# A Perceiver layer on one core: the last unit's maxima turned to rows on TensorE, the last tile's attention quarters one step apart, the last pair's groups together, and the maximum later in its step

## The chip, the cores and the metric

The kernel runs on one core of a Trainium2 chip. The metric is device time in microseconds (us) of one execution, as the median of several. The core's engines are named as the profile names them: PE is TensorE's matmul, PEld its weight load (which runs beneath the matmul before it), DVE is VectorE, ACT is ScalarE, POOL is GpSimd, and SP is the engine that issues most DMAs here. PSUM is the memory into which PE writes.

## The reference

The layer takes x (16 batches of 64 rows, 256 wide) and a context of 16 batches of 1601 rows, 256 wide. Three residual parts follow one another:

```python
x = x + xattn(layernorm(x), ctx)   # 16 query heads and 8 key groups of 128, self and cross attention
x = x + attn(layernorm(x))         # 16 heads of 16, blocks of 8 rows, causal; then a gated feed-forward
x = x + ffn(layernorm(x))          # ternary weights, 704 wide
```

Most of the arithmetic is the cross attention of the first part, for each batch and each key group:

```python
kvx = cond @ w_kv_x.T; kx, vx = split(kvx)
kx  = ln(kx)                              # per head of 128
xout = softmax(qx @ kx.T / sqrt(128)) @ vx
cat  = concat([core, xout])               # core: self attention over the 64 rows
out  = fp8(clip(bf16(cat / proj_smooth))) @ wproj.T * scale
```

The second part quantises activations per row to 8 bits (`act_quant`: the row's largest magnitude, scale by 127, round) and weights to -1, 0, 1. Its attention works in blocks of 8 rows over 16 heads.

## The kernel before

**Tiles and units.** The 1024 rows of x are 8 tiles i of 128 rows (two batches each), held in SBUF for the whole run as `xr[i]`. The cross attention of a tile is cut into four units: two halves hh of the key groups (four groups each) by two batches bb. So there are 32 units, n = 0 to 31. A unit walks over the context in 13 chunks c of 128 rows (the last 65).

**A unit.** Per chunk, `project` makes the keys `ps_k` (4 matmuls, L487), ACT squares them, `squares` sums the squares per head on DVE (L498) and takes the inverse root on POOL, `normalise` scales into `kn` (DVE, L506), `transpose_k` turns them on PE (`tr_kx`, L520) and evicts them with the norm's weights into `kT` (ACT, L522), and `score` multiplies with the queries (8 matmuls, `s`, L533). The scores have context rows on the partitions and 4 x 128 queries along the row. ACT copies them, scaled, to an SBUF tile `P` (L538), and DVE keeps the running maximum of all chunks in `M` (L541 for the first chunk, L543 after it). There is one buffer of M, and 19 of P, in the pool `pp`.

After the last chunk, `maximum` finds each query's maximum over the context rows, which lie on the partitions: PE transposes M in four blocks (`tr_m`, L550), DVE reduces each (`red`, L552), and DVE scales it (L562). The result stands one query per partition, but it is wanted along the row and on every partition. So SP writes `red` to a DRAM tile `rowd` (L557), and `maximum_in` reads it back to all partitions as `mx` (L567). Then `exponent` subtracts mx from each P (DVE, L571) and takes the exponential in place (ACT, L575), and `accumulate` multiplies P with the context rows and a column of ones (10 matmuls, `acc`, L590). After its last chunk four tiles of the accumulator are divided by their sums into `pq` (L600 to 604), and `turn_contexts` transposes those into the pair's `pc` (`tr_pc`, L613).

**Behind the units.** When both batches of (i, hh) are done, `pair_out` multiplies with the value weights (`po_x`, L645), for two groups gp one after the other; for each it rounds on DVE to fp8 (L654 and the helper at L192 to L197, `cat` L265) and projects (`po_p`, L278), adding into `xr[i]` (L282). Between the two groups it waits for `gap` steps and loads the second group's weights. When tile i's x is complete, `last_parts` runs the second and third residual part of that tile: norm, `act_quant`, the 8-bit qkv product (`ps_qk`, `ps_v`), rope (r1, r2), a transpose to `qkT`, then four *quarters* (two row halves j of heads by two sets c), each with a masked query tile `qm` (L802), scores `sc` (L809), mask and maximum and exponential (L814 to 821), `tr_p` (L825), its ACT copy `pT` (L827), and the value product `av` (L831) into `cx`; then `po_o`, the gated feed-forward (`ps_g`, `ps_u`, `po_d`), and the ternary one (`pgu`, L906, `sgc`, `hd`, and `po_f`, L924), and the output DMA (L931). qm and pT share 2 buffers (`b2b`), sm3 has part of 3 (`b2`).

**What sets the order.** The program is emitted by a hand-written planner. Each piece of work is put on a heap at a step and a rank, `spawn(step, rank, generator)` or `at(step, rank, function)`. The heap hands out by step, then by rank; a generator that yields k continues k steps later at its rank. Every engine runs its own instructions in the order of emission, and waits are placed by dependency. SP's DMAs are also issued in that order. A unit's base is 13n. Within one step s:

- rank 0 the loads, rank 0.5 `maximum_in` (at base + 17), rank 1 normalise
- rank 2 project, rank 2.5 `last_parts` and the quarters, **rank 3.4 `maximum`** (at base + 15)
- rank 3.5 accumulate (c at base + c + 20), rank 4 self attention, queries and norms of the coming tile, rank 4.2 squares
- rank 5 score (c at base + c + 2), rank 6 transpose_k, rank 7 pair_out, rank 8 exponent (c at base + c + 18)

All transposes, scores, projections and quarters share three PSUM tiles of the tag "s". Tile i starts `last_parts` at step 52i + 92, the last one at 52i + 79; its quarters stand three steps apart.

Of the kernel before, what the change touches and what calls it, by code (L numbers as in the profile page):

```python
# [14 lines left out]
F32 = mybir.dt.float32  # L15
# [8 lines left out]
P = 128  # L24
# [34 lines left out]
def body(tc, ctx, a):  # L59
# [28 lines left out]
    def at(step, rank, fn):  # L88
        def once():
            fn()  # L90
            yield 1

        spawn(step, rank, once())
# [89 lines left out]
    def quant_tile():  # L183
        return qp.tile([P, 512], F32, tag="q_y", name="q_y")
# [74 lines left out]
    def to_cat(y, exact):  # L259

        cat = qp.tile([P, 4, P], F32R if exact else F32, tag="cat", name="cat")

        def emit(t, m):
            for g in range(2):
                V.tensor_tensor(  # L265
                    cat[:, 2 * g : 2 * g + 2, :].rearrange("p h (b s) -> p b h s", b=2),
                    t[:, 256 * g : 256 * (g + 1)].rearrange("p (b h s) -> p b h s", b=2, h=2),
                    m[:, 256 * g : 256 * (g + 1)].rearrange("p (b h s) -> p b h s", b=2, h=2), ALU.subtract,
                )

        fp8_round(y, emit)
        return cat
# [191 lines left out]

    def unit(i, hh, bb, base):
        b = 2 * i + bb
        st = {"cxT": {}, "cxN": {}, "ps": {}, "ss": {}, "rs": {}, "kn": {}, "kT": {}, "P": {}, "pT": {}}
        pair = pairs.setdefault((i, hh), {})

# [85 lines left out]
        def out_rows(r):  # L555
            d = dram.tile([4, P], F32, tag="rowd", name="rowd", bufs=4)
            nc.sync.dma_start(out=d.rearrange("g q -> q g"), in_=r)  # L557
            return d

        def maximum():  # L560
            r = turned("M", ALU.max)
            V.tensor_scalar(r, r, C_ATT, None, ALU.mult)  # L562
            st["mxd"] = out_rows(r)

        def maximum_in():
            st["mx"] = one.tile([P, 4, P], F32, tag="mx", name="mx", bufs=2)
# [49 lines left out]
        for c in range(NC):  # L616
# [7 lines left out]
            at(base + c + 17, 0, lambda c=c: load_N(c))  # L624
            at(base + c + 18, 8, lambda c=c: exponent(c))
            at(base + c + 20, 3.5, lambda c=c: accumulate(c))
        at(base + 15, 3.4, maximum)
        at(base + 17, 0.5, maximum_in)
        for k in range(2):
            at(base + 33, 1.8 + 4.4 * k, lambda k=k: turn_contexts(k))  # L630

    def pair_out(i, hh, gap):


        pair = pairs[i, hh]
        wv = piece("wvx", (v2, w_kvT[:, :, 1024 + 512 * hh : 1536 + 512 * hh]))
        yield 1
        w_p = weights("wproj", 4 + 2 * hh)
        yield 1
        for gp in range(2):  # L640
            po = s_tile("po_x")
            for g2 in range(2):
                g = 2 * gp + g2
                for k in range(2):
                    PE.matmul(  # L645
                        po[:, g2 * 256 : (g2 + 1) * 256], lhsT=v2(wv)[:, k, g * D : (g + 1) * D],
                        rhs=pair["pc"][:, k, g].rearrange("p b q -> p (b q)"), start=k == 0, stop=k == 1,
                    )
            y = quant_tile()
            for g2 in range(2):  # L650
                h0 = 24 + 8 * hh + 4 * gp + 2 * g2
                yg = y[:, g2 * 256 : (g2 + 1) * 256].rearrange("p (b h s) -> p b h s", b=2, h=2)
                pg = po[:, g2 * 256 : (g2 + 1) * 256].rearrange("p (b h s) -> p b h s", b=2, h=2)
                V.tensor_tensor(yg, pg, rsc[:, h0 : h0 + 2].unsqueeze(1).unsqueeze(3).to_broadcast([P, 2, 2, S]), ALU.mult)  # L654
            cat = to_cat(y, True)
            yield 1
            project_out(i, cat, w_p)
            if gp == 0:
                yield gap - 3
                w_p = weights("wproj", 5 + 2 * hh)  # L660
                yield 2
# [48 lines left out]
    def b2(name):  # L710
        return one.tile([P, 512], F32, tag="b2", name=name, bufs=3)

    def b2b(name):
        return one.tile([P, 512], F32, tag="b2b", name=name, bufs=2)
# [12 lines left out]
    def act_quant(src, w, j):  # L727


        am = small.tile([P, 1], F32, tag="am", name="am")  # L730
        V.tensor_reduce(am, src, AX.X, ALU.max, apply_absolute_value=True)
        V.tensor_scalar(am, am, 1e-5, None, ALU.max)
        sc = small.tile([P, 1], F32, tag="asc", name="asc")
        V.reciprocal(sc, am)
        V.tensor_scalar(sc, sc, 127.0, None, ALU.mult)
        f = small.tile([P, 1], F32, tag="fsc", name="fsc")
        V.tensor_scalar(f, am, wmean[:, j : j + 1], 1.0 / 127.0, ALU.mult, ALU.mult)
        u = b2("aq_u")
        V.tensor_scalar(u[:, :w], src, sc, 127.0, ALU.mult, ALU.min)
        V.tensor_scalar(u[:, :w], u[:, :w], -128.0, ROUND, ALU.max, ALU.add)  # L740
        q = b1("aq_q", BF16)
        V.tensor_scalar(q[:, :w], u[:, :w], ROUND, None, ALU.subtract)
        yield 1
        tr = tr_tile("tr_aq", BF16)
        for k in range(w // P):
            PE.transpose(tr[:, k * P : (k + 1) * P], q[:, k * P : (k + 1) * P], identb)
        qT = b1("aq_t", BF16)
        V.tensor_copy(qT[:, :w], tr[:, :w])
        yield 1
        return qT.rearrange("p (k t) -> p k t", k=4), f  # L750
# [3 lines left out]
    def last_parts(i, start):  # L754
# [41 lines left out]
        yield 1  # L796
        cx = one.tile([P, H], F32, tag="cx3", name="cx3")

        def quarter(j, c):

            qm = b2b("qm").rearrange("p (h t) -> p h t", h=4)
            V.tensor_tensor(  # L802
                qm, qkT[:, j * P : (j + 1) * P].unsqueeze(1).to_broadcast([P, 4, P]),
                hmask[:, 4 * c : 4 * c + 4].unsqueeze(2).to_broadcast([P, 4, P]), ALU.mult,
            )
            yield 1
            sc = s_tile("sc3")
            for h in range(4):
                PE.matmul(  # L809
                    sc[:, h * P : (h + 1) * P], lhsT=qm[:, h, :], rhs=qkT[:, 256 + j * P : 256 + (j + 1) * P],  # L810
                    start=True, stop=True,
                )
            sm = b2("sm3").rearrange("p (h t) -> p h t", h=4)
            V.tensor_tensor(  # L814
                sm, sc.rearrange("p (h t) -> p h t", h=4), cmask.unsqueeze(1).to_broadcast([P, 4, P]), ALU.add
            )
            mx = small.tile([P, 4], F32, tag="mx3", name="mx3")
            V.reduce_max(mx, sm, axis=AX.X)
            V.tensor_tensor(sm, sm, mx.unsqueeze(2).to_broadcast([P, 4, P]), ALU.subtract)
            yield 1  # L820
            A.activation(sm, sm, AF.Exp, scale=0.25)
            yield 1
            tr = tr_tile("tr_p3")
            for h in range(4):
                PE.transpose(tr[:, h * P : (h + 1) * P], sm[:, h, :], ident)  # L825
            pT = b2b("pT3")
            A.copy(pT, tr)  # L827
            yield 1
            av = s_tile("av")
            for h in range(4):  # L830
                PE.matmul(  # L831
                    av[:, h * 17 : (h + 1) * 17], lhsT=pT[:, h * P : (h + 1) * P], rhs=vx[:, 8 * j + 4 * c + h, :],
                    start=True, stop=True,
                )
            av3 = av[:, 0 : 4 * 17].rearrange("p (h d) -> p h d", h=4)
            rv = small.tile([P, 4], F32, tag="rv3", name="rv3")
            V.reciprocal(rv, av3[:, :, 16])
            o = 128 * j + 64 * c
            V.tensor_tensor(
                cx[:, o : o + 64].rearrange("p (h d) -> p h d", h=4), av3[:, :, 0:16],  # L840
                rv.unsqueeze(2).to_broadcast([P, 4, 16]), ALU.mult,
            )

        s0 = start + 9
        for n in range(4):
            spawn(s0 + 3 * n, 2.5, quarter(n // 2, n % 2))
        yield 3 * 3 + 5
        to = ternary_piece(1536, 512).rearrange("p (k o) -> p k o", k=2)
        yield 1
        cT, f = yield from act_quant(cx, H, 1)  # L850
# [101 lines left out]
    for i in range(NT):  # L952
        base = 52 * i
        for hh in range(2):
            for bb in range(2):
                unit(i, hh, bb, base + 26 * hh + 13 * bb)
            spawn(base + 26 * hh + 13 + 34 - 2, 7, pair_out(i, hh, 5 if i < NT - 1 or hh == 0 else 3))
        ln0, sa0, qx0 = SCHEDULE[i] if i in SCHEDULE else (
            base - 23, [base + o for o in (-16, -4, 8, 22)], [base + o for o in (-14, -5, 12, 20)]
        )  # L960
        spawn(ln0, EX, ln_tile(i))
        for p in range(4):
            spawn(sa0[p] - 2, EX, self_attention(i, p))
            spawn(qx0[p] - 2, EX, queries(i, p))
        l0 = base + (92 if i < NT - 1 else 79)
        spawn(l0, 2.5, last_parts(i, l0))
    spawn(60, 5.7, ternary())
    order = [(kind, p) for p in range(4) for kind in ("wq", "wkv", "wqx", "wproj")]
# [75 lines left out]
```

## Time and profile before

Three runs took 2778.85, 2780.6 and 2781.8 us, the median is 2780.6. The profiled execution took 2779.82 us, of which the span from first to last instruction is 2777.7; its mean TensorE clock was 0.978 of full.

| | us |
|---|---|
| median of 3 runs | 2780.6 |
| profiled execution, its span | 2779.82, 2777.7 |
| PE busy, first 100 us | 79.08 |
| PE busy, 100 to 620 | 485.34 of 520 |
| PE busy, 2709.6 to 2739.8 (the last tile's four quarters) | 17.19 of 30.2, clock 0.58 |
| `acc` L590, 4160 matmuls | 807.6 |
| `ps_k` L487, 1664 matmuls | 796.5 |
| `s` L533, 3328 matmuls | 445.9 |
| `M` L543, 384 operations on DVE | 263.4 |
| `mx` subtraction L571, 416 operations on DVE | 282.1 |

A row with a line number sums what the program does there over all 32 units. A stretch such as 100 to 620 is counted from the start of the span. Where a row of the profile is followed by an arrow (`tr_m <- DVE M`), the instruction on the left stood idle until the one on the right had ended.

### The profile page before, as it was taken

The page shows a single profiled execution, that of the slowest core. Times are in us where ns is not written, and L with a number is a line of the kernel's source. Part 1 is how long each engine was busy: PE and PEld are TensorE (multiplying, and loading weights), DVE is VectorE, ACT ScalarE, POOL GpSimd, SP SyncE. Part 2 cuts the span into 40 slices and gives each one's busy share as a digit, 9 for nine tenths or more (in the row PEclk, how much of TensorE's full clock was granted, in tenths as well). Part 3 has the DMA queues.
Part 4 walks back from the last instruction along what each step waited for, and adds up shares of the span by engine and source line. Part 5 has one row for each costly group of instructions (what it writes and reads, how often), then busy time and mean ns, then how long its engine had stood idle before and what let it go on. Part 6 is the DMA issues. An engine that isn't in the chain of part 4 may idle for free.

```text
span 2777.7 us, 41656 instructions
## 1 busy us (share of the span) xinstructions
PE 2623.7 (94%) x14848; PEld 2033.2 (73%) x14848; DVE 1896.1 (68%) x4643; ACT 1418.9 (51%) x2556; POOL 851.0 (31%) x1248
## 2 busy tenths in 40 slices
PE   7899989999999999999999999999999999999885
PEld 4577767768777787777777687777877778777774
DVE  7777756767666766667677676676766676765643
ACT  4555534445565455644556445654556545574421
POOL 3333323332333323333332333323333332333100
PEclk9999999999999999999999999999999999999986
DMA  7556634334344334434344343443434433443220
GB/s 253 187 173 193 229 123 134 101 109 124 110 146 142 117 102 122 133 113 135 117 127 132 97 130 114 145 133 107 120 113 142 142 120 105 118 129 82 64 90 14
DMA packets 232351, 353.34 MB, mean 127 GB/s; under 512 B 43952, under 2 KB 172752, under 8 KB 232144
## 3 DMA queue, kind: packets, MB, share of 16 engines
q1 hardware_dynamic: 231856, 350.52, 40.4%
q8 instruction: 117, 1.92, 0.3%
q14 instruction: 90, 0.74, 0.1%
q10 hardware_dynamic: 288, 0.17, 0.0%
HBM read 327.74 MB, written 22.87 MB: 126 GB/s over the span
## 4 chain that ended last, share of the span: by engine, by line
PE 69%; DVE 17%; POOL 6%; ACT 3%; DMA 3%; issue 2%; SPq 0%; ACTq 0%; POOLq 0%; DVEq 0%
PE acc L590 20%; PE ps_k L487 19%; PE s L533 10%; PE tr_kx L520 5%; DVE ss L498 2%; POOL rs L160 2%; PE po_p L278 2%; DVE M L543 2%; PE po_x L645 2%; DVE P L571 2%; DVE kn L506 1%; POOL rsx L160 1%; PE pgu L906 1%; POOL ve L159 1%; PE ps_q L324 1%
## 5 line engine op out<-in xcount | busy, mean ns | idle before, releaser
L590 PEld LDWEIGHTS acc<-ctxN,P 128*128 128x128 f32 (+1 forms) x4160 | 713.5, 192 | 186.2 <-issue 105.0
L590 PE MATMUL acc<-ctxN,P 128*128 128x257 f32 (+5 forms) x4160 | 807.6, 342 | 8.8 <-ACT pq L602 8.8
L487 PE MATMUL ps_k<-wkx,ctxT 128*128 128x512 f32 (+1 forms) x1664 | 796.5, 599 | 5.8 <-DVE wkx L941 5.4
L159 POOL TENSOR_SCALAR ve<-ss 128x4 f32<-128x4 f32 (+2 forms) x432 | 218.9, 507 | 1493.2 <-DVE ss L498 1275.0
L575 ACT ACTIVATE P<-P 128x512 f32<-128x512 f32 (+1 forms) x416 | 261.2, 630 | 579.7 <-DVE P L571 579.3
L533 PE MATMUL s<-qx,kT 128*128 128x128 f32 (+1 forms) x3328 | 445.9, 277 | 25.4 <-ACT kT L522 8.2
L160 POOL TENSOR_TENSOR rsx<-ve,nhalf 128x4 f32<-128x4 f32 (+1 forms) x416 | 437.7, 1052 | 31.6
L533 PEld LDWEIGHTS s<-qx,kT 128*128 128x128 f32 (+1 forms) x3328 | 406.4, 188 | 44.7 <-ACT kT L522 13.0
L487 PEld LDWEIGHTS ps_k<-wkx,ctxT 128*128 128x128 f32 (+1 forms) x1664 | 282.2, 189 | 204.2 <-issue 194.6
L543 DVE TENSOR_TENSOR M<-s,M 128x512 f32<-128x512 f32 (+1 forms) x384 | 263.4, 686 | 225.4 <-ACT P L538 222.9
L492 ACT ACTIVATE sq<-ps_k 128x512 f32<-128x512 f32 (+1 forms) x416 | 248.3, 597 | 311.3 <-PE ps_k L487 299.6
L498 DVE TENSOR_REDUCE ss<-sq 128x4 f32<-128x512 f32 (+1 forms) x416 | 283.0, 680 | 138.2 <-ACT sq L492 136.5
L522 ACT ACTIVATE kT<-tr_kx,vec 128x512 f32<-128x512 f32 (+1 forms) x416 | 315.9, 759 | 31.8 <-PE tr_kx L520 31.8
L538 ACT ACTIVATE P<-s 128x512 f32<-128x512 f32 (+1 forms) x416 | 246.5, 592 | 147.1 <-PE s L533 145.1
L506 DVE TENSOR_TENSOR kn<-ps_k,rsx 128x512 f32<-128x512 f32 (+1 forms) x416 | 282.8, 680 | 14.9 <-POOL rsx L160 14.9
L571 DVE TENSOR_TENSOR P<-P,mx 128x512 f32<-128x512 f32 (+1 forms) x416 | 282.1, 680 | 10.7 <-DMA mx<-rowd 10.7
L520 PE MATMUL tr_kx<-ident,kn 128*128 128x128 f32 (+1 forms) x1664 | 247.6, 272 | 28.1 <-DVE kn L506 16.7
L520 PEld LDWEIGHTS tr_kx<-ident,kn 128*128 128x128 f32 (+1 forms) x1664 | 192.7, 143 | 38.1 <-DVE kn L506 12.7
L178 DVE TENSOR_SCALAR qn<-qn,mv,rs 128x128 f32<-128x128 f32 x256 | 76.1, 341 | 83.2 <-POOL rs L172 83.1
L160 POOL TENSOR_TENSOR rs<-ve,nhalf 128x4 f32<-128x4 f32 (+2 forms) x144 | 113.7, 790 | 8.3
L278 PE MATMUL po_p<-wproj,cat 128*128 128x256 f32 x512 | 85.5, 310 | 5.5 <-DVE cat L265 5.4
L168 DVE BATCH_NORM_STATS2 st<-qn 128x6 f32<-128x128 f32 x256 | 63.8, 271 | 37.7 <-ACT qn L334 37.7
(187 smaller groups left out, 2599.2 us busy)
## 6 DMA issues: line engine op xcount, KB each, us to landing
wproj<-wproj SPq DMA_DIRECT2D x120, 512.0 KB
ctxT<-in_ctx SPq DMA_DIRECT2D x192, 256.0 KB
ctxN<-in_ctx_n SPq DMA_DIRECT2D x384, 128.0 KB
wq<-wq SPq DMA_DIRECT2D x56, 512.0 KB
wkv<-wkv SPq DMA_DIRECT2D x56, 512.0 KB
wqx<-wqx SPq DMA_DIRECT2D x56, 512.0 KB
mx<-rowd SPq DMA_DIRECT2D x32, 256.0 KB
wvx<-in_w_kv_x SPq DMA_DIRECT2D x16, 512.0 KB
```

What stands on the lines that cost most here:

```text
L160: GP.tensor_tensor(out, ve[:n, :g], nhalf[:n, :g], ALU.pow)
L487: PE.matmul(ps[:n, :], lhsT=st["cxT"][c // 2][:, k, o : o + n], rhs=wkx[:, k, 512 * hh : 512 * (hh + 1)], start=k == 0, stop=k == 1,)
L492: A.activation(sq[:n], ps[:n], AF.Square)
L498: mark["ss"] = V.reduce_sum(ss[:n], st["ss"].pop(c)[:n].rearrange("p (g d) -> p g d", g=4), axis=AX.X)
L506: mark["kn"] = V.tensor_tensor(kn[:n].rearrange("p (g d) -> p g d", g=4), ps[:n].rearrange("p (g d) -> p g d", g=4), rs[:n].unsqueeze(2).t ...
L520: PE.transpose(tr[:, g * P : g * P + n], kn[:n, g * D : (g + 1) * D], ident[:n, :n])
L522: A.activation(kT[:, :, 0:n], tr.rearrange("p (g t) -> p g t", g=4)[:, :, 0:n], AF.Identity, bias=col("kxln_b"), scale=col("kxln_w"),)
L533: PE.matmul(ps[:n, g * P : (g + 1) * P], lhsT=kT[:, g, 0:n], rhs=qxs[i, hh][:, bb, 2 * g : 2 * g + 2, :].rearrange("p h s -> p (h s)"), st ...
L543: mark["M"] = V.tensor_tensor(st["M"][:n], ps[:n], st["M"][:n], ALU.max)
L571: ins = V.tensor_tensor(pc[:n], pc[:n], st["mx"][:n].rearrange("p g q -> p (g q)"), ALU.subtract)
L575: A.activation(pc[:n], pc[:n], AF.Exp)
L590: PE.matmul(ps, lhsT=pc[:n, g * P : (g + 1) * P], rhs=cx[:n, o : o + w], start=g == 2 and c == 0, stop=c == NC - 1 and (g, o) in ((2, 0), ...
```

## The change

It has six parts.

1. In all units `maximum` moves from rank 3.4 to 6.5 of its step: behind accumulate, self attention, squares, score and transpose_k.
2. In the last unit (n = 31) the maxima do not go through DRAM. PE transposes each column of `red`, broadcast along the row, which gives the maxima along the row on every partition (`tr_mb`, four transposes), and ACT copies them to `mx`. `maximum_in` is not emitted for it.
3. The last pair's `pair_out` takes `gap` None: the value products of both groups come one behind the other, both weights are loaded up front, and rounding and projection of both follow in the same step. It ends the generator there.
4. The last tile's quarters stand one step apart, not three, and its qm, sm3 and pT3 are taken from the 19 buffers of P.
5. `last_parts` of tile 6 starts at 52i + 80 rather than 92, that of tile 7 at 52i + 74 rather than 79.
6. In `act_quant` the small factor `fsc` is written after q, not before u.

```diff
@@ unit
+        last = b == B - 1 and hh == 1
@@ maximum
-            st["mxd"] = out_rows(r)
+            if not last:
+                st["mxd"] = out_rows(r)
+                return
+
+            tr = tr_tile("tr_mb")
+            for g in range(4):
+                PE.transpose(tr[:, g * P : (g + 1) * P], r[:, g : g + 1].to_broadcast([P, P]), ident)
+            st["mx"] = one.tile([P, 4, P], F32, tag="mx", name="mx", bufs=2)
+            A.copy(st["mx"], tr.rearrange("p (g q) -> p g q", g=4))
@@
-        at(base + 15, 3.4, maximum)
-        at(base + 17, 0.5, maximum_in)
+        at(base + 15, 6.5, maximum)
+        if not last:
+            at(base + 17, 0.5, maximum_in)
@@ pair_out: group(gp) and rounded(gp, po) hold what the loop held
+        if gap is None:
+            ws = [w_p, weights("wproj", 5 + 2 * hh)]
+            pos = [group(gp) for gp in range(2)]
+            for gp in range(2):
+                project_out(i, rounded(gp, pos[gp]), ws[gp])
+            return
         for gp in range(2):
...
+            cat = rounded(gp, group(gp))
             yield 1
             project_out(i, cat, w_p)
@@ act_quant
-        f = small.tile([P, 1], F32, tag="fsc", name="fsc")
-        V.tensor_scalar(f, am, wmean[:, j : j + 1], 1.0 / 127.0, ALU.mult, ALU.mult)
         u = b2("aq_u")
...
         V.tensor_scalar(q[:, :w], u[:, :w], ROUND, None, ALU.subtract)
+        f = small.tile([P, 1], F32, tag="fsc", name="fsc")
+        V.tensor_scalar(f, am, wmean[:, j : j + 1], 1.0 / 127.0, ALU.mult, ALU.mult)
@@ last_parts
+        def room(name):
+            return b2b(name) if i < NT - 1 else pp.tile([P, 512], F32, tag="P", name=name)
+
@@ quarter
-            qm = b2b("qm").rearrange("p (h t) -> p h t", h=4)
+            qm = room("qm").rearrange("p (h t) -> p h t", h=4)
-            sm = b2("sm3").rearrange("p (h t) -> p h t", h=4)
+            sm = (b2 if i < NT - 1 else room)("sm3").rearrange("p (h t) -> p h t", h=4)
-            pT = b2b("pT3")
+            pT = room("pT3")
@@
-        s0 = start + 9
+        s0, gap = start + 9, 3 if i < NT - 1 else 1
         for n in range(4):
-            spawn(s0 + 3 * n, 2.5, quarter(n // 2, n % 2))
-        yield 3 * 3 + 5
+            spawn(s0 + gap * n, 2.5, quarter(n // 2, n % 2))
+        yield 3 * gap + 5
@@ the plan
-            spawn(base + 26 * hh + 13 + 34 - 2, 7, pair_out(i, hh, 5 if i < NT - 1 or hh == 0 else 3))
+            spawn(base + 26 * hh + 13 + 34 - 2, 7, pair_out(i, hh, 5 if i < NT - 1 or hh == 0 else None))
-        l0 = base + (92 if i < NT - 1 else 79)
+        l0 = base + {NT - 2: 80, NT - 1: 74}.get(i, 92)
```

More of the change, by code (lines that the diff above doesn't have):

```diff
@@ L639, in pair_out, with group @@
         yield 1
-        for gp in range(2):
+        def group(gp):
             po = s_tile("po_x")
@@ L648, in pair_out, with rounded @@
                     )
+            return po
+        def rounded(gp, po):
             y = quant_tile()
@@ L654, in pair_out @@
                 V.tensor_tensor(yg, pg, rsc[:, h0 : h0 + 2].unsqueeze(1).unsqueeze(3).to_broadcast([P, 2, 2, S]), ALU.mult)
-            cat = to_cat(y, True)
+            return to_cat(y, True)
+        if gap is None:
[4 more added lines that the diff above has]
+            return
+        for gp in range(2):
+            cat = rounded(gp, group(gp))
             yield 1
```

## The prediction, made before the changed kernel was run

> **What bounds the kernel now.** I read the page's shares first, then the slices of part 2, the waits by engine, busy time by stretch, and the chain of the last 180 us.
>
> ```profile
> PE 2623.7 (94%) x14848; PEld 2033.2 (73%) x14848; DVE 1896.1 (68%) x4643; ACT 1418.9 (51%) x2556; POOL 851.0 (31%) x1248
> PE   7899989999999999999999999999999999999885
> PEclk9999999999999999999999999999999999999986
> ```
>
> PE is the bound: it idles 154 us in all, and the thin slices are the first and the last three. No other engine is near full, so only PE's gaps, its slow clock and the serial end can be won. Stretches (us; busy time of PE, PEld, DVE, ACT and POOL with their counts; granted clock; DMA share; GB/s):
>
> ```profile
> 620.00:2560.00 1940.00, 1891.96 (x10946) 1477.39 (x10945) 1347.60 (x3299) 1052.63 (x1880) 618.01 (x901) 1.00 0.40 122
> 2560.00:2618.00 58.00, 57.99 (x346) 46.61 (x346) 42.17 (x80) 30.64 (x53) 15.40 (x19) 1.00 0.23 71
> 2618.00:2638.00 20.00, 11.22 (x76) 10.39 (x75) 7.48 (x20) 4.44 (x9) 0.00 (x0) 0.86 0.34 93
> 2638.00:2676.00 38.00, 37.25 (x188) 31.34 (x188) 16.71 (x47) 10.63 (x20) 0.88 (x3) 0.85 0.18 57
> 2676.00:2695.00 19.00, 12.94 (x74) 11.43 (x73) 10.77 (x29) 2.17 (x5) 0.80 (x2) 0.88 0.38 122
> 2695.00:2778.00 83.00, 47.96 (x208) 38.12 (x207) 31.80 (x82) 13.96 (x27) 4.55 (x9) 0.64 0.10 33
> ```
>
> Up to 2618 PE is full at full clock; after that it stands 8.8 us, and the mean clock of every later stretch is below full. The chain shows the first cause, and the serial quarters at the end:
>
> ```profile
> 2618.30 0.44 PE tr_m L550 x4
> 2618.73 0.46 PE acc L590 x4
> 2620.11 10.11 DMA rowd<-red
> 2630.24 4.38 DMA mx<-rowd
> 2634.63 0.70 DVE P L571
> ...
> 2715.81 1.11 PE tr_p L825 x4
> 2716.93 1.71 PE sc L809 x8
> 2718.63 1.53 PE av L831 x8
> ```
>
> PE's and VectorE's waits name what the maximum costs elsewhere (us in total, times, longest):
>
> ```profile
> PE tr_m L550 <- DVE M L543: 26.5, 14, 3.3
> DVE P L571 <- DMA mx<-rowd: 10.7, 2, 9.5
> SPq L567 <- DMA rowd<-red: 252.6, 31, 10.5
> ```
>
> So tr_m holds PE 26.5 us over 32 units, while the trip of the maxima through DRAM is hidden in all but two.
>
> [...]after the 8.8 us gap ten acc matmuls take 2.80 us in the chain against 1.75 before it; recovery took until about 2648.5.[...] here a subtraction without its maxima left VectorE 7.48 us busy of 20.[...]
>
> **The change part by part**, on the profiled execution (span 2777.7, 2.1 us around it: 2779.8; the median is 0.8 above that).
>
> *Maximum later in its step (all units).* tr_m is now emitted behind the step's accumulate, score, transpose_k and their evictions, instead of ahead of accumulate. Nothing is added or removed. The waits fall in two classes by the place of the unit: 7 units wait 3.28 us or a little less, where a last_parts instruction (h, waiting for POOL) stands ahead of M on VectorE, and 7 wait 0.62. In the second class tr_m now comes when M is done: 7 x 0.6 = 4.2 gained. In the first, M's lateness is only met by the next PE instructions: score waits for an eviction, tr_kx for a slot behind it, tr_m for a slot of self-attention. I allow 7 x 0.5 = 3.5 of the possible 7 x 3.3 = 23. Odd units gain a short new wait behind hd, about 0.4 in 8 of them: 3 lost. Against this stands the trip: red, its DMA, SP's wait for it and the mx load all come later, by 2.75 us (odd units), 3.85 (second class), 5.1 (first class). The slack from mx's landing to the first exponent is 1.3 to 6 us (15 once), so in six of the first class VectorE waits 2 to 4 us, 17 in all, and in the first units 1 to 4. Queued behind that subtraction are rope's r2, r1 and the q_y of self-attention, for which PE's next transposes wait, and the M and kn of the running chunk. VectorE is 68% busy and catches up; I charge PE a third, 6 us. Sum: 4.2 + 3.5 - 3 - 6 = 1.3 lost. Bounds: 20 gained (both classes vanish, no echo), 25 lost (every VectorE wait reaches PE).
>
> *Last unit's maxima on TensorE, and tile 6's last_parts 12 steps earlier.* From tr_m to the last acc were 56.9 us. Out: the 8.8 us gap; about 6 us of half clock behind it (2638 to 2648.5 held matmuls at up to double time); tile 6's quarters and gate matmuls, 7.9 (sc 1.7, av 2.3, tr_p 0.4, ps_g and ps_u 3.4), which now run before tr_m. In: 5.1 us of pgu that stood after acc; a wait at the turn of units, about 2, for pq behind exponentials and table loads on ACT, and 0.35 at tr_xn; four transposes and the wait for red and for ACT's copy, 2.25 (priced by tr_m 0.44, red 0.69, an ACT copy 0.6, hand-overs). 56.9 - 22.7 + 9.7 = 43.9, 13.0 less. Work moved ahead of tr_m costs 7.35 at full clock. Acc ends 5.65 earlier.[...] by another count of the same rows it is 7.1. The copy reads PSUM and waits on no DMA in flight.
>
> *Last pair's groups together.* From acc's end to tile 7's final x were 20.0: first rounding begins 4.89 after acc, then project_out 1.78, 2.78 of pgu, the second po_x 1.73, more pgu, the second rounding. Now both po_x come first. 4.89, plus 1.75 since po_f (2.6) stands ahead, two roundings of 3.33 on VectorE, the last po_p 1.45 and x 0.5: 15.25, say 15.4. Gain 4.6. Both weights are loaded up front and land well before; if a buffer holds one, its load is late: at most the 4.6.
>
> *Last tile's quarters one step apart.* From qkT to the last cx were 30.1 us, four rounds of about 6.6 behind one another, in which PE was busy 17.2 and VectorE 11.6 (busy time of that stretch). Now four quarters overlap and their tiles come from the 19 buffers that P no longer needs. Floor: VectorE's 11.6 plus the first sc and the last tr_p, pT, av (1.2 + 1.1 + 0.6 + 1.9) = 16.4. At half clock PE needs 4 x (1.71 + 1.11 + 1.53) = 17.4, and up to 20 with handing over; I take 19. Gain 11, bounds 5.5 (three PSUM slots of "s" serialise them) and 13.7.
>
> *Tile 6 out of the end.* Its pgu and po_f delayed tile 7's last_parts by about 0.25 at xa, 0.65 at sq, 0.2 at am and 1.0 at tr_qk: 2.1 gained. The other start (79 to 74 steps) only keeps order: x's last sum sets when it begins. Moving fsc costs nothing, it is one 128x1 operation off PE's path.
>
> Sum: -5.65 - 4.6 - 11 - 2.1 + 1.3 = -22.05. 2779.8 - 22.0 = 2757.8, plus 0.8 for the median: 2758.6, say **2759**.
>
> **The rivals.** (a) *tr_m's stalls vanish wholly*: all 26.5 us of L550 less the edge cases, 20; for it, PE has ten more matmuls to do before tr_m; against, M's lateness is VectorE's queue, which meets other PE waits. 2779.8 - 23.35 - 20 + 0.8: 2737. (b) *The tail gives half*: quarters 5.5, acc end 2.8, pair_out 3, tile 6 1 = 12.3; for it, three PSUM slots and a clock of 0.64 there; against, PE is half idle in the stretch. With the main stage's 1.3 lost: 2769 to 2770. (c) *Main stage eats the tail*: 17 to 28 us lost against 23.35 gained: 2774 to 2785, centred on no change; for it, the later trip, at the upper part of its bounds. (d) *Slower*: the first exponent of each unit waits for the later mx, and VectorE's order passes that to M, kn and PE. It decides from 0.9 us of PE time per unit (29 over 32 units, against 23.35 + 5.6); at 1.2 us it is 38 us, 2780.6 - 23.35 + 38 = 2795. For it, 3 to 5 us later against slack down to 0.2; against, the slack of most odd units is over 3 and PE runs on scores and projections.
>
> **How the numbers follow.** Forecast 0.60, (a) 0.14, (b) 0.15, (c) 0.07, (d) 0.04. About 0.2%, 5.6 us, is what a measurement of this kernel can tell from no change. Faster: forecast, (a), (b) and a little of (c), 0.90; same 0.06; slower 0.04. The range runs from 2739 (nearly (a)) to 2774 (all of (b), the edge of (c)); this takes in quarters at their bounds and a main stage from 18 gained to 16 lost.
>
> **What would show it.** Right: no rowd and mx issue for the last unit; no PE gap of 8 us near 2618; the last acc at about 2671, x's last sum at 2686, the quarters in under 20 us, and the span's end near 2756; tr_m's waits at about half, with new ones at s and tr_kx. New rows of VectorE P waiting for mx, some 17 to 25 us, would confirm the later trip. Wrong: quarters still 6 us apart, or PE idle in 620 to 2560 up by more than 15 us.

## The result: slower, and where the time went

The changed kernel took 2797.48 us (median of 6 runs, 2796.07 to 2803.18), the kernel before 2779.18 beside it. The ratio is 1.0067, 95% interval 1.0054 to 1.0080: slower by 18 us where 22 us faster had been forecast. Run again later (f1_changed_again below) it took 2783.59, ratio 1.0004 (0.9992 to 1.0016): no gain either, and 14 us away from the first result. That difference became part of the answer.

Both profiles have the same matmuls, but for the four of tr_mb (and a few records that the trace lacks). The shares and the slices of PE's clock on the page after the change:

```profile
PE 2634.0 (94%) x14844; PEld 2032.2 (73%) x14852; DVE 1890.6 (68%) x4643; ACT 1419.0 (51%) x2559; POOL 837.3 (30%) x1248
PEclk9999989999999999999999999999999999999996
```

PE is busy 10 us longer for the same work, and the slice from 349.5 to 419.3 us has a mean clock of 0.88, with 0.50 from 356.8 to 367.1. Four stretches of the changed kernel follow, in the columns of those shown before: the main stage, from the last tr_m to the last acc, from there to the last x, and the rest.

```profile
620.00:2560.00 1940.00, 1883.92 (x10809) 1466.54 (x10814) 1333.23 (x3288) 1038.23 (x1862) 601.59 (x890) 0.99 0.41 122
2668.00:2714.00 46.00, 44.40 (x257) 37.24 (x255) 18.58 (x50) 16.76 (x29) 0.80 (x2) 0.96 0.37 118
2714.00:2729.00 15.00, 10.41 (x52) 8.86 (x52) 8.84 (x25) 1.58 (x4) 0.00 (x0) 0.89 0.43 136
2729.00:2795.70 66.70, 35.46 (x173) 26.70 (x174) 30.16 (x77) 12.65 (x24) 4.55 (x9) 0.68 0.06 18
```

In 620 to 2560 PE ran 10809 matmuls where it had run 10946, in nearly the same busy time: it stood a little more, and what it did was slower, at a mean clock of 0.99 where it was 1.00. From 2668 on it is quicker than before. The last tr_m starts at 2668.3 in the chain, where it was 2618.3, and the span ends 18.0 later. So the end gave back 32 of 50 us:

```profile
2668.30 0.44 PE tr_m L551 x4
2668.74 1.09 PE acc L599 x6
2669.82 0.61 PE tr_mb L570 x4
...
2671.34 0.61 DVE P L580
...
2754.87 0.66 PE tr_p L851 x4
2755.53 2.42 PE av L857 x16
```

The two DMA lines that stood between tr_m and the first P are gone; 3 us, not 16, lie between them. Of the four serial rounds of tr_p, sc and av the chain has one sc, one tr_p and one run of av left. Stretch by stretch, from the timelines (us):

| stretch | before | forecast | after |
|---|---|---|---|
| last tr_m, start | 2618.1 | 2626.8 | 2668.1 |
| tr_m to the last acc | 56.9 | 43.9 | 45.8 |
| acc to the last x | 19.9 | 15.4 | 15.2 |
| x to qkT | 14.6 | 12.5 | 13.2 |
| qkT to the last cx | 30.1 | 19 | 16.1 |
| cx to the output tile | 35.3 | 35.3 | 34.6 |

The whole error lies in the first row. The waits of PE and VectorE name it. Before:

```profile
PE tr_kx L520 <- DVE q_y L444: 7.3, 8, 2.1
```

After:

```profile
PE tr_kx L521 <- DVE q_y L444: 29.7, 9, 4.5
PE tr_kx L521 <- ACT qx L343: 14.9, 6, 2.5
```

```profile
DVE P L580 <- DMA mx<-rowd: 54.1, 22, 5.4
DVE M L542 <- PE tr_m L551: 34.1, 20, 2.0
```

tr_m's 26.5 us are gone, and what came is larger: PE's wait for q_y was 7.3 in 8 places and is 29.7 in 9, its wait for qx is new, and VectorE's wait for mx was 10.7 in 2 and is 54.1 in 22. Unit 22 is one such place. Before, VectorE's timeline (start, duration, what, in brackets the idle time before it and its releaser) had no wait, and PE's hardly one:

```profile
1914.44 0.68 DVE L571 TENSOR_TENSOR P<-P,mx 128x512 f32<-128x512 f32 x1
1915.04 1.83 DVE L784 TENSOR_TENSOR r<-qk,shp 128x256 f32<-128x256 f32 x2
```

```profile
1918.06 0.66 PE L520 MATMUL tr_kx<-ident,kn 128*128 128x128 f32 x4 [0.81 <-DVE q_y L444]
```

After:

```profile
1952.72 0.69 DVE L580 TENSOR_TENSOR P<-P,mx 128x512 f32<-128x512 f32 x1 [4.24 <-DMA mx<-rowd]
1953.33 0.75 DVE L807 TENSOR_TENSOR r<-qk,shp 128x256 f32<-128x256 f32 x2
1954.19 0.69 DVE L812 TENSOR_TENSOR r<-r,r 128x512 f32<-128x512 f32 x1
1954.80 0.75 DVE L444 TENSOR_TENSOR q_y<-po_s,rsc 128x256 f32<-128x256 f32 x2
```

```profile
1955.27 1.11 PE L521 MATMUL tr_kx<-ident,kn 128*128 128x128 f32 x4 [4.07 <-DVE q_y L444]
1956.18 3.62 PE L488 MATMUL ps_k<-wkx,ctxT 128*128 128x512 f32 x4
```

The subtraction waits 4.24 us for its maxima. rope's products and q_y stand behind it in VectorE's order and run at once when it is done; PE's next transpose needs the PSUM tile that q_y frees. When PE goes on, four ps_k matmuls take 3.62 us where they took 1.88 before, because the clock has fallen (the last figures but two are the granted clock, 0.52 and then 0.99):

```profile
1954.00:1961.00 7.00, 5.73 (x12) 3.39 (x13) 5.40 (x13) 1.94 (x4) 0.00 (x0) 0.52 0.04 12
1961.00:1968.00 7.00, 7.00 (x41) 5.07 (x39) 4.72 (x13) 3.84 (x8) 1.81 (x4) 0.99 0.20 53
```

The sum agrees. At the start of acc of unit 29 the changed kernel is 46.2 us late (2506.0 and 2552.2); 18.6 of them are there by unit 6. From 60 us to there PE's idle entries add up to 104.2 us, where they were 81.1: 23 more. In the clock records half clock (0.50 granted) lasts 88.7 us, where it was 34.1: 54.6 us more, worth up to half of that, 27. Together that is 50, with an upper price for the clock.

### The profile page after: what moved, and what is told of

Its sections match the earlier page's. It is cut to its first block, busy times and chain, and to the rows that moved or that the text cites. A ratio compares the mean times of both kernels' runs of the same rounds, so it can differ in the third digit from the quotient of the medians.

```text
span 2795.7 us, 41656 instructions
## 1 busy us (share of the span) xinstructions
PE 2634.0 (94%) x14844; PEld 2032.2 (73%) x14852; DVE 1890.6 (68%) x4643; ACT 1419.0 (51%) x2559; POOL 837.3 (30%) x1248
## 4 chain that ended last, share of the span: by engine, by line
PE 63%; DVE 16%; DMA 8%; POOL 6%; ACT 4%; issue 2%; SPq 0%; ACTq 0%; POOLq 0%; DVEq 0%
PE ps_k L488 19%; PE acc L599 17%; PE s L534 9%; PE tr_kx L521 5%; DMA rowd<-red 5%; POOL rs L160 2%; DMA mx<-rowd 2%; DVE ss L499 2%; DVE P L580 2%; PE po_p L278 2%; DVE kn L507 2%; DVE M L544 2%; PE po_x L656 2%; POOL rsx L160 2%; DVE st L168 1%
## 5 line engine op out<-in xcount | busy, mean ns | idle before, releaser
L488 PE MATMUL ps_k<-wkx,ctxT 128*128 128x512 f32 (+1 forms) x1664 | 814.0, 609 | 5.7 <-DVE wkx L968 5.5
L159 POOL TENSOR_SCALAR ve<-ss 128x4 f32<-128x4 f32 (+2 forms) x432 | 207.5, 481 | 1532.3 <-DVE ss L499 1462.7
L534 PE MATMUL s<-qx,kT 128*128 128x128 f32 (+1 forms) x3328 | 446.0, 277 | 22.9 <-ACT kT L523 11.4
L580 DVE TENSOR_TENSOR P<-P,mx 128x512 f32<-128x512 f32 (+1 forms) x416 | 282.4, 681 | 54.2 <-DMA mx<-rowd 54.1
L521 PE MATMUL tr_kx<-ident,kn 128*128 128x128 f32 (+1 forms) x1664 | 252.2, 275 | 68.7 <-DVE q_y L444 29.7
L507 DVE TENSOR_TENSOR kn<-ps_k,rsx 128x512 f32<-128x512 f32 (+1 forms) x416 | 282.9, 680 | 19.9 <-POOL rsx L160 19.9
```

The lines of the kernel that those rows point to most:

```text
L488: PE.matmul(ps[:n, :], lhsT=st["cxT"][c // 2][:, k, o : o + n], rhs=wkx[:, k, 512 * hh : 512 * (hh + 1)], start=k == 0, stop=k == 1,)
L507: mark["kn"] = V.tensor_tensor(kn[:n].rearrange("p (g d) -> p g d", g=4), ps[:n].rearrange("p (g d) -> p g d", g=4), rs[:n].unsqueeze(2).t ...
L521: PE.transpose(tr[:, g * P : g * P + n], kn[:n, g * D : (g + 1) * D], ident[:n, :n])
L534: PE.matmul(ps[:n, g * P : (g + 1) * P], lhsT=kT[:, g, 0:n], rhs=qxs[i, hh][:, bb, 2 * g : 2 * g + 2, :].rearrange("p h s -> p (h s)"), st ...
L580: ins = V.tensor_tensor(pc[:n], pc[:n], st["mx"][:n].rearrange("p g q -> p (g q)"), ALU.subtract)
```

## The experiments

Theory 1 is the later maxima: their trip through DRAM ends after the first exponent's turn, VectorE's fixed order carries the wait to q_y, PE stands, and its clock falls behind the standstill. Theory 2 is tr_m's late place itself: tr_m then holds a PSUM tile that tr_kx wants, and frees the one buffer of M later. Theory 3 is that a part of the change at the end reaches back. The kernels are named by their labels. The e runs were taken on one chip beside the kernel before (median 2778.35), the f runs on a second (2782.24), the g runs on a third (2778.25), the k runs on a fourth (2779.91), so differences between letters are read better from the ratios:

| run | edit | us | ratio to before, 95% |
|---|---|---|---|
| e1_rank34 | changed, rank 3.4 | 2752.77 | 0.9903 (0.9880 to 0.9926) |
| e2_only_late | before, rank 6.5 | 2801.27 | 1.0080 (1.0054 to 1.0105) |
| e3_exp_later | changed, first exponent later | 2745.07 | 0.9874 (0.9853 to 0.9895) |
| e4_rank37 | changed, rank 3.7 | 2741.41 | 0.9862 (0.9839 to 0.9886) |
| f1_changed_again | changed | 2783.59 | 1.0004 (0.9992 to 1.0016) |
| f2_rank37_exp_later | both edits of e3, e4 | 2737.34 | 0.9837 (0.9817 to 0.9858) |
| f3_rank37_gap3 | e4, quarters three steps apart | 2755.23 | 0.9907 (0.9891 to 0.9924) |
| f4_all_on_tensor | changed, no trip in any unit | 2757.86 | 0.9913 (0.9896 to 0.9930) |
| g0_rank37_again | as e4 | 2741.41 | 0.9867 (0.9847 to 0.9888) |
| g1_no_pair_together | e4, pair in turn | 2745.64 | 0.9884 (0.9857 to 0.9910) |
| g2_last_by_dram | e4, last unit by DRAM | 2754.18 | 0.9908 (0.9888 to 0.9929) |
| g3_tile6_at_90 | e4, tile 6 at 90 steps | 2737.12 | 0.9846 (0.9828 to 0.9865) |
| k2_longer_trip | e1, a second DRAM tile | 2762.36 | 0.9938 (0.9918 to 0.9958) |
| k1_best | f2, tile 6 at 90 steps | 2734.61 | 0.9836 (0.9822 to 0.9851) |

**The move alone, and all but the move.**

```diff
-        at(base + 15, 6.5, maximum)
+        at(base + 15, 3.4, maximum)
```

> The changed kernel with maximum back at rank 3.4; all else of the change stays. Theory 1 (the later trip of the maxima makes VectorE wait at the first exponent, q_y behind it holds PE, and the idle time halves PE's clock) and theory 2 (tr_m's place on PE itself costs the time: its stall comes back at tr_kx and the first M copy waits for it) both expect the 43 us lost before the last tr_m to return and the 25 us gained at the end to stay: 2754, within 3. Theory 3 (a tail part, such as tile 6's work 12 steps earlier, costs part of it) expects 2760 or more.

```profile
PE tr_m L551 <- DVE M L544: 23.4, 12, 3.3
PE tr_kx L521 <- DVE q_y L444: 7.0, 7, 2.1
```

2752.77: theories 1 and 2 stand, theory 3 is out at this end. tr_m's stall is back, no VectorE wait for mx is left, and q_y is no later than before. Against the first result the move costs 44.7 us, and the rest of the change gains 25.6.

The kernel before, with the same line the other way round (rank 3.4 to 6.5):

> The kernel before with maximum moved to rank 6.5 and nothing else of the change. Theories 1 and 2: the whole loss of the main stage, 2779 + 43 = 2822, within 5. Theory 3: less than 2810. VectorE's wait for mx over 50 us, PE's wait for q_y about 30.

2801.27, 23 us slower and not 43. The direction is as expected, the size is half, below the line drawn for theory 3. But up to about unit 29 both programs issue the same instructions in the same order, except for the 128x1 fsc, and there this one is only 26.4 us late, the changed one 46.2. That the rest of the change makes the difference is thus unlikely. The waits, VectorE's and PE's, are smaller:

```profile
DVE P L571 <- DMA mx<-rowd: 46.7, 14, 8.3
```

```profile
PE tr_kx L520 <- DVE q_y L444: 21.6, 8, 3.6
```

One of the 14 is the last unit's, 8 us and at the end, as before. SP issues the mx load a mean of 8.94 us after rowd here, 9.77 in the changed kernel's profile. The changed kernel was therefore run again:

> The changed kernel once more, unaltered. The kernel with only maximum moved lost 22 us, the changed one about 43 in the same stretch, though up to unit 29 both issue the same instructions in the same order. If that spread belongs to single executions[...], this comes anywhere from 2775 to 2800; if it belongs to the changed kernel, 2795 to 2800 with 80 to 90 us of half clock before 2615.

2783.59, 14 us less than at first, and with 78.5 us of half clock from 60 us to the first acc of unit 29. So 2795 to 2800 isn't the changed kernel's own time. Against this run the move costs 31 us, not 45. Its 12 executions (2776.15 to 2790.91) and the first six (2796.07 to 2803.18) do not overlap, so it isn't chance from one execution to the next. The trip, from the issue of rowd to that of the mx load, is 8.77 us there.

```profile
DVE P L580 <- DMA mx<-rowd: 31.9, 11, 4.1
```

```profile
PE tr_kx L521 <- DVE q_y L444: 21.1, 8, 3.7
```

With the trip one microsecond shorter, VectorE's waits are 22 us less. This is one profile against another; what made the first one's trip longer wasn't tried, and the chip of the first result isn't known.

**The wait's victims moved in front of it.** The first exponent of each unit is put behind self attention of the next step:

```diff
-            at(base + c + 18, 8, lambda c=c: exponent(c))
+            at(base + c + 18 + (c == 0), 4.1 if c == 0 else 8, lambda c=c: exponent(c))
```

> The changed kernel, maximum at rank 6.5, with only the first exponent of each unit moved nearly a step later (base + 19, rank 4.1), so that it stands behind rope and q_y on VectorE. Theory 1: VectorE's wait for mx falls from 54 us to under 10, PE's wait for q_y from 30 to under 8, no half clock after it: 2757 to 2767. Theory 2: nothing changes for tr_m, 2793 to 2800.

2745.07: 52 us less than the changed kernel at first, and 38.5 less than its second run, in which the trip was as long as here (8.77 and 8.75 us). tr_m stands at the same late place.

```profile
DVE P L580 <- DMA mx<-rowd: 1.2, 2, 0.7
```

```profile
PE tr_kx L521 <- DVE q_y L444: 3.8, 8, 2.1
PE tr_kx L521 <- ACT qx L343: 14.9, 6, 2.5
```

PE's wait for ACT's qx is still there in full. So theory 2 falls as the cause of the loss, and the late place is even worth some 8 us against rank 3.4 on the same chip once nothing waits for the trip (all of it, if the exponent's own move gains nothing). Theory 1 had expected 2757 to 2767, without this gain. The late place does keep some slow clock: half clock from 60 us to unit 29 is 47.8 us here, 34.1 in e1_rank34 and 88.7 in the changed kernel, so about 14 of the changed kernel's 54.6 us more do not come from the trip.

**No trip at all.**

```diff
-        last = b == B - 1 and hh == 1
+        last = True
```

> Maximum at rank 6.5, and the maxima turned to rows on TensorE in all 32 units, so that none goes through DRAM. Theory 1 (the trip is what costs): no VectorE wait for a DMA, PE's wait for q_y back to about 7 us, and 31 x 4 transposes more, 14 us of PE: 2745 (the run with the later exponent) + 14 = 2759, within 6. Theory 2 (tr_m's place): 2797 + 14 = 2811.

```profile
DVE M L542 <- PE tr_m L551: 33.0, 19, 2.0
```

```profile
PE tr_kx L521 <- DVE q_y L444: 7.6, 8, 2.1
```

2757.86. VectorE no longer waits for mx, PE's wait for q_y is as before the change, and VectorE's M still waits for tr_m as long as in the changed kernel: M's single buffer is not the cause. The difference to e3_exp_later is 12.8 us (10.8 by the ratios), near the 14 of transposes that had been put down for it.

**The trip lengthened at tr_m's old place.** tr_m stands where it does in e1_rank34, and its waits on PE are the same (23.5 in 12); only a DRAM tile comes between:

```diff
-        at(base + 15, 6.5, maximum)
+        at(base + 15, 3.4, maximum)
...
-            return d
+            e = dram.tile([4, P], F32, tag="rowe", name="rowe", bufs=4)
+            st["hop"] = (e, d)
+            return e
...
+            at(base + 17, 0.4, hop)      # dma_start(out=e, in_=d)
```

> The changed kernel with maximum back at rank 3.4 (2752.8 without more), but the maxima go from rowd to a second DRAM tile and only from there to mx: a longer trip at the old place of tr_m. Theory 1: the trip alone is enough; an extra transfer of 3 to 5 us is what the move of tr_m had added, so VectorE waits 30 us or more for mx, PE for q_y 20 or more, and 2775 to 2800 results. Theory 2 in its weaker form (the loss needs tr_m and M's buffer in their late place as well): 2752 to 2760.

2762.36: 9.6 us slower than e1_rank34 on another chip. The executions do not overlap (2759.09 to 2767.52, 2750.38 to 2757.05), the intervals of the ratios touch. It is less than expected of theory 1 and a little more than of theory 2. The trip is 12.55 us from rowd to the mx load against 8.74, and VectorE's waits show that even this mostly fits into the slack:

```profile
DVE P L586 <- DMA mx<-rowe: 12.3, 8, 3.8
```

```profile
PE tr_kx L521 <- DVE q_y L444: 10.1, 8, 2.5
```

So a longer trip alone is enough to lose time, about as much as VectorE waits for it. The late tr_m adds more than these 3.8 us: 5.1 by the prediction's reading, in the units hit worst. Set against one another, VectorE's waits for mx before the first acc of unit 29, and how much later than e1_rank34 (2507.4) that acc starts: 11.3 us of waits and 9.0 later (k2), 33.4 and 25.0 (e2), 31.9 and 33.2 (f1), 52.4 and 44.8 (the changed kernel). PE pays 0.75 to 1.04 us for each microsecond that VectorE waits. In the last three this is net of tr_m's stalls, which they no longer have. Counted from e3_exp_later instead (2498.5, 1.2 us of waits), which has none either, they pay 1.05 to 1.37: 33.9 us for 32.2 (e2), 42.1 for 30.7 (f1), 53.7 for 51.2 (the changed kernel).

**A place between.** Behind accumulate, ahead of the rest:

```diff
-        at(base + 15, 6.5, maximum)
+        at(base + 15, 3.7, maximum)
```

> The changed kernel with maximum at rank 3.7: behind accumulate (1.75 us of matmuls) but ahead of self attention, squares, score and transposes. Theory 1: the trip starts at most 1.8 us later than at 3.4, which the slack holds in nearly all units, and tr_m's stalls shrink from 26.5 us to about 10: 5 to 12 us faster than with rank 3.4, 2742 to 2749. Theory 2: tr_m behind accumulate costs a share of the 43 us, slower than with rank 3.4.

2741.41, just under theory 1's range, and the same again in a later job (g0_rank37_again):

> The changed kernel with maximum at rank 3.7 once more, as the base of the three beside it: 2741 if the chip is like the others, a ratio to before of 0.984 to 0.989.

```profile
PE tr_m L551 <- DVE M L544: 9.2, 6, 1.5
```

```profile
DVE P L580 <- DMA mx<-rowd: 3.4, 2, 2.9
```

The ten matmuls of acc cover 1.75 of the 3.28 us, and the trip still ends in time in nearly all units. Half clock from 60 us to unit 29 is 20.5 us in both profiles, the lowest so far.

Both edits together:

> Maximum at rank 3.7 and the first exponent nearly a step later. If both take away the same wait for the maxima, they don't add: 2738 to 2743, as with rank 3.7 alone. If moving the exponent has a gain of its own (rope and q_y freed from behind a subtraction), 2732 to 2737.

2737.34, between the two expectations, its interval overlapping that of rank 3.7 alone: a gain of the exponent's own of some 4 us is not shown.

**The parts at the end,** each taken back on the base of rank 3.7. The quarters (gap 3, and b2b and b2 for their tiles):

> Maximum at rank 3.7, the last tile's quarters three steps apart and in their own buffers again, all else changed. The stretch from qkT to the last cx goes back from about 16 us to about 30, so 2741.4 + 14 = 2755 (the prediction had put the part at 11: 2752). If the order of steps doesn't matter there, because nothing else stands between, 2741 to 2745.

2755.23. The stretch from qkT to the last cx is 30.07 us again, from 17.42 in e4 and 16.2 in g0. The part is worth 11 to 14 us (by the ratios to before, by the times).

The pair's groups in turn (gap 3, tile 7 at 79 steps):

> Rank 3.7, with the last pair's groups one behind the other again (gap 3, and tile 7's last_parts at 79 steps, which that order needs). The prediction's 4.6 us: acc's end to x goes from 15.4 back to about 20, so the base + 4.6. If the second po_x and its weights were never what x waited for, the base within 1.5.

2745.64. From acc's end to x takes 18.07 us, where g0 has 15.17: 2.9 of the 4.6 forecast. The medians differ by 4.2, but the intervals overlap.

The last unit by DRAM (`last = False`):

> Rank 3.7, with the last unit's maxima through DRAM again. PE runs dry for about 9 us and at half clock behind it (6 us), while tile 6's work, which had filled some of that, now lies earlier: the base + 12 to 17. If tile 6's pgu matmuls fill the gap and keep the clock, the base + 4 to 7.

2754.18, 12.8 more than the base. From tr_m to the last acc are 54.56 us, where g0 has 44.20, with the two transfers in the chain:

```profile
2612.22 7.99 DMA rowd<-red
2620.22 5.25 DMA mx<-rowd
```

Tile 6 at 90 steps:

> Rank 3.7, with tile 6's last_parts at 90 steps, ten later and nearly where it was. Its work returns into the stretch from tr_m to the last x and the head of tile 7's last_parts: the base + 2 to 5 (2.1 for the head, the rest where it delays acc and x). If it was only moved and PE has the same sum to do, the base within 1.5.

2737.12: 4 us faster, a sign that neither expectation had, with overlapping intervals. In the profiles tr_m starts 6.0 earlier, acc ends 8.2 earlier and x 9.4, and the head of tile 7's last_parts takes 16.91 us rather than 13.25. So its work costs 3.7 at the head, and the same work ahead of tr_m costs more. The earlier start thus looks like a small loss; it is not settled. Moving fsc and the earlier start of tile 7 were not tried alone.

**The parts found, together:** rank 3.7, the first exponent later, tile 6 at 90 steps.

> Rank 3.7, the first exponent nearly a step later, and tile 6's last_parts at 90 steps. If the 4 us of each add to 2741.4: 2733. If they share their gain: 2736 to 2739.

2734.61, 45 us less than the kernel before in the same job, ratio 0.9836 (0.9822 to 0.9851). Against f2 its gain is within the spread.

## Why the prediction was wrong

The step that failed is the trip's term in "Maximum later in its step": "I charge PE a third, 6 us". The path was seen rightly; its price was not. In place of the 1.3 us that this part was to lose, the last tr_m came 50.0 us later, of which 7.35 had been put down for work moved ahead of it: about 43 us lost. The price was wrong in three ways, each with its measured number.

- *How long VectorE waits.* Put down: 17 us in six units of the first class, 1 to 4 in each of the first units. Measured: 23.9 in those six (3.1 to 4.7 each), and 2.1 to 5.4 in units 0, 1, 2, 4 and 5, 22 in all, which the sum then left out; unit 2 had waited 1.3 us in the trace of before already. Slack was read from one execution and taken as fixed; the trip in the recorded profile was 9.77 us, in that of before 9.35.
- *What of it reaches PE.* Put down: a third. Measured: in these six units PE's wait for q_y rose from 0.8 to between 2.9 and 4.5, 22.9 us against 4.9: three quarters of VectorE's wait. That VectorE is busy only 68% did not help: q_y was not late for want of time, it stood behind the waiting instruction in order. The prediction itself had named r2, r1 and q_y there; the price for what is queued behind a wait should have been near the wait itself.
- *What follows the idle time.* Put down: nothing, in the forecast and also in the bound of 25 lost, "every VectorE wait reaches PE". Measured: 54.6 us more at half clock, up to 27 us, some three quarters of it from the trip, as e3_exp_later shows. The clock had been read out of the trace for the end of the kernel, and was not asked of the new waits in the middle.

The gains of that part had nearly the right size. tr_m's small stalls went; the large ones came back at tr_kx as 2.5 us each ("7 x 0.5" of 3.28; measured 0.8 each). With the trip made harmless, the late place is worth some 8 us against the 4.7 that the sum had before its charge of 6.

One sign of being wrong had been named that did not show: PE idle in 620 to 2560 up by more than 15 us. It rose there from 48.0 to 56.1 only. As much again and more, 12.4, came in 60 to 620, in the first units, and slow clock isn't idle time.

The rival (d) had the mechanism: the first exponent, VectorE's order, PE, though the wait reached PE through q_y, which it doesn't name, more than through M and kn. It was given 0.04. The point from which it decides, 0.9 us per unit, was passed: 43 us over 32 units, 1.3 each. That its 2795 is so near 2797 is in part luck: the second run of the same kernel, 2783.59, lies in the range of (c), with the same mechanism. Its weight went wrong through the mean over units: the slack of odd units, which spoke against it, does not matter when units of the other kind lose about 5 us each (26 us over the five from unit 10 to unit 26), and those up to unit 6 another 18.6.

The end was nearly right. acc's stretch was 45.8 for 43.9, the pair 15.2 for 15.4, tile 6's part 1.4 for 2.1, and the quarters 16.1 for 19: the half clock put down for them didn't last, the stretch has a mean clock of 0.82 where it was 0.58. With 0.7 that no part had claimed this is 32.0 us for 30.7, less the work moved ahead of tr_m, 7.35 put down and 6.0 seen in g3. That this move as a whole might cost rather than gain, as g3 suggests, was not foreseen.

## What to carry to other kernels

When an instruction is moved later, follow the longest thing that starts from it, a trip through memory above all, to the instruction that waits for its end, and charge everything queued behind that one with the whole wait; VectorE's busy share of 68% was no cover here. A stall that is moved may come back in a place where the wait costs more: compare its length with the slack of the worst kind of unit, not with the mean. If PE then stands, look for a lower clock behind it: here half clock lasted 54.6 us longer, up to 27 us lost. And repeat a result before explaining its last 14 us.

## What the runs showed of the hardware

- The length of one wait did not decide whether half clock (0.50 granted) came with it. In the kernel before, PE waited 3.28 or 3.29 us at tr_m in six units and 2.86 in one. The 7 us behind three of these waits (at 907.6, 1566.2 and 2224.8 us) have a mean clock of 0.76, those behind the other four have 1.00. In the changed kernel a stretch at 0.50 came with all six of PE's 2.49 us waits at tr_kx for qx, and with six of its seven waits there for q_y of 2.90 us or more; in the 7 us behind the seventh, 2.90 us long, the clock was 1.00. What decides it was not shown.
- The same program's trip from rowd to mx took 9.77 us on average in one profile of the changed kernel and 8.77 in the other, and the kernel's time was 14 us apart with it, while the kernel before, whose slack covers the trip in all but two units, had medians from 2778.25 to 2782.24 on four chips.
- Four transposes of a broadcast column (0.27 us each, overlapping to 0.61 in the chain) and an ACT copy of 128x512 (0.58 us) turned the maxima to a row on every partition, where the trip through DRAM took 10.11 and 4.38 us in the last unit before.
